# A differential-attention kernel: half of the groups subtracted before the transposes, their magnitudes summed on ScalarE

## The chip, the cores and the metric

The kernel runs on one core of one Trainium2 chip. The metric is the device time of one execution in microseconds. A core has five engines that work through their own queues in order: TensorE (PE in the profile, with its weight loads as PEld), VectorE (DVE), ScalarE (ACT), GpSimd (POOL) and the queue engine SyncE (SP).

## The reference

The input x is 8 sequences of 512 tokens with 128 features. Differential attention with 16 heads of 8 features is followed by a layer norm and a mixture of 8 experts of which each token uses 2. The part that the change touches is the attention:

```
s1 = q @ k1.T * SCALE ; s2 = q @ k2.T * SCALE        # causal, per head
attn = softmax(s1) - sigmoid(lambda) * softmax(s2)
denom = maximum(sum(abs(attn), axis=-1), 1e-6)
out = (attn / denom) @ v
x = layernorm(x + out @ Wo.T)
...
x = layernorm(x + moe(layernorm(x) * gamma + beta))
```

## The kernel before

**Units.** A unit is 32 queries of one sequence `b`; a sequence has 16 units `j`, and unit `j` sees L = 32 (j+1) keys. Four heads make a group, and a group's four heads times 32 queries fill the 128 partitions. So a unit has four groups of [128, L] scores, each twice: set 0 for k1 and set 1 for k2. The tile `et` holds the exponentials of all groups and both sets, as `et[:, g, set, :L]`.

**What happens to a unit.** `scores` puts the scores into PSUM (L342, and a causal mask by L351). `maxima` takes the negated row maximum on VectorE (L364, L372). `exps` takes the exponential on ScalarE and, with it, the row sums (L382). `combine` then does two things for each group: VectorE forms max(e1, c·e2) and sums it along the row into `big` (L408; the elementwise result goes to a tile `junk` that nobody reads), and GpSimd scales e2 by -c in place (L418). Here c is the ratio of the two row sums times sigmoid(lambda), made in `ratios`. The sum of magnitudes needs no subtraction, because |a - b| = 2 max(a, b) - a - b. `transposes` turns both tensors of a group on TensorE into the same place in PSUM, where the second is added to the first (L436), so that the difference comes out of the transposes. `evacuate` copies it to SBUF on ScalarE (L456, L458), and `times_v` multiplies with the values (L468). When four units of a block are done, `reciprocals` forms the denominators from `sums` and `big`.

**Pieces and slots.** A unit with L up to 256 is early: it has two slots (two groups with both sets each) and two pieces, groups (0, 1) and (2, 3). A later unit has four slots (two groups, one set) and four pieces of one group each. A slot is one round of the schedule.

**The order.** The order on each engine is written out by hand, in `round_of`, with manual scheduling: the program issues instructions in exactly this order. A round, for the slot `now` whose scores are there and the slot `ahead` whose scores are next, issues: the product with v of units that are ready; the scores of `ahead`; the evacuation of the transposes of the round before; ScalarE's waiting steps (`on_act`: the tanh of an expert, L815, or the copy of its output, L860, with a store); the maxima of `now`; the transposes of the piece combined the round before; VectorE's waiting steps; the combining of the next piece; the exponentials of `now`; late VectorE steps; then projection, normalisation and routing steps and up to two expert steps (L850, L870), as a pace allows. Score tiles have two buffers in PSUM, the transposes' tile `pt` has one, `et` has three.

**Experts.** They run in chunks of 5 to 7 blocks, some rounds behind the attention; from the third sequence on expert steps stand between the attention's steps.

Of the kernel before, what the change touches and what calls it, by code (L numbers as in the profile page):

```python
# [20 lines left out]
def kernel(  # L21
# [15 lines left out]
    nc = tc.nc  # L37
# [96 lines left out]
    with ExitStack() as actx:  # L134
# [28 lines left out]
        won = aw.tile([P, D], F32, name="won")  # L163
        wo_sb = aw.tile([P, 4, D], F32, name="wo_sb")
        slam = aw.tile([P, NG], F32, name="slam")
        slam1 = aw.tile([P, NG], F32, name="slam1")
        hm = aw.tile([P, 4], F32, name="hm")
        hms = aw.tile([P, 4], F32, name="hms")
# [1 line left out]
        i4 = aw.tile([P, 4, Q], BF16, name="i4")  # L170
        mk = aw.tile([P, Q], BF16, name="mk")
        junk = aw.tile([P, T], F32, name="junk")

        xts = {}

# [47 lines left out]
            )  # L223
        nc.scalar.activation(slam, slam, AF.Sigmoid)
        nc.vector.tensor_scalar(slam1, slam, 1.0, None, ALU.add)
        for h in range(4):
            nc.vector.tensor_scalar_mul(wo_sb[:, h, :], won, hm[:, h : h + 1])

# [86 lines left out]
        class Unit:  # L315


            def __init__(self, b, j, blk):
# [11 lines left out]
                self.et = ep.tile([P, NG, 2, T], F32, tag="et", name=f"et_{b}_{j}")  # L330
                self.aT = self.c2 = None

            def scores(self, slot):
                gp, s = slot
                qb, kT, _ = qkv[self.b]
                L, j = self.L, self.j
                sc = ps_s.tile([P, 2, T], F32, tag="sc", name=f"sc_{self.b}_{j}_{gp}_{s}")
                for si in range(2) if s is None else (s,):
                    lo = 0 if s is not None else si * (T // 2)
                    for gi in range(2):  # L340
                        r = slice(32 * (2 * gp + gi), 32 * (2 * gp + gi) + 32)
                        nc.tensor.matmul(  # L342
                            sc[:, gi, lo : lo + L],
                            lhsT=qb[r, j].rearrange("p h q -> p (h q)"),
                            rhs=kT[r, si, :L],
                            start=True,
                            stop=False,
                        )
                    for gi in range(2):
                        r = slice(32 * (2 * gp + gi), 32 * (2 * gp + gi) + 32)  # L350
                        nc.tensor.matmul(  # L351
                            sc[:, gi, lo + L - Q : lo + L],
                            lhsT=i4[r].rearrange("p h q -> p (h q)"),
                            rhs=mk[r],
                            start=False,
                            stop=True,
                        )
                return sc
# [31 lines left out]
            def ratios(self):  # L390

                sums, jj = self.blk["sums"], self.jj
                c1 = sp.tile([P, NG], F32, tag="c1", name=f"c1_{self.b}_{self.j}")
                nc.vector.tensor_mul(c1, sums[:, 0, jj, :], slam)
                self.c2 = sp.tile([P, NG], F32, tag="c2", name=f"c2_{self.b}_{self.j}")
                r2 = sp.tile([P, NG], F32, tag="r2", name=f"r2_{self.b}_{self.j}")
                nc.vector.reciprocal(r2, sums[:, 1, jj, :])
                nc.vector.tensor_mul(self.c2, c1, r2)

            def combine(self, piece):  # L400

                if self.c2 is None:
                    self.ratios()
                L = self.L
                for g in piece:
                    nc.vector.scalar_tensor_tensor(  # L408
                        junk[:, :L],
                        self.et[:, g, 1, :L],  # L410
                        self.c2[:, g : g + 1],
                        self.et[:, g, 0, :L],
                        ALU.mult,
                        ALU.max,
                        accum_out=self.blk["big"][:, self.jj, g : g + 1],
                    )
                for g in piece:
                    nc.gpsimd.tensor_scalar(  # L418
                        self.et[:, g, 1, :L],
                        self.et[:, g, 1, :L],  # L420
                        self.c2[:, g : g + 1],
                        -1.0,
                        ALU.mult,
                        ALU.mult,
                    )

            def widths(self):
                return [min(P, self.L - P * kb) for kb in range(self.n)]

            def transposes(self, piece):  # L430

                pt = ps_t.tile([P, 4, P], F32, tag="pt", name=f"pt_{self.b}_{self.j}_{piece[0]}")
                for x_, g in enumerate(piece):
                    for kb, kw in enumerate(self.widths()):
                        for k in range(2):
                            nc.tensor.matmul(  # L436
                                pt[:kw, x_ * self.n + kb, :],
                                lhsT=self.et[:, g, k, kb * P : kb * P + kw],
                                rhs=ident,
                                is_transpose=True,  # L440
                                start=(k == 0),
                                stop=(k == 1),
                            )
                return pt

# [30 lines left out]
        def block_tasks(b, i, blk):  # L476
# [7 lines left out]
            def reciprocals():  # L484
                s["oraw"] = op.tile([P, JT, P], F32, tag="oraw", name=f"oraw_{n}")
                nc.scalar.copy(s["oraw"], blk["po"])

                dg = bp.tile([P, JT, NG], F32, tag="dg", name=f"dg_{n}")
                nc.vector.tensor_mul(
                    dg, blk["sums"][:, 0], slam1.unsqueeze(1).to_broadcast([P, JT, NG])  # L490
                )
                nc.vector.scalar_tensor_tensor(dg, blk["big"], 2.0, dg, ALU.mult, ALU.subtract)
                nc.vector.scalar_tensor_tensor(
                    dg, blk["sums"][:, 0], 1e-6, dg, ALU.mult, ALU.max
                )
                rd = bp.tile([P, JT, NG], F32, tag="rd", name=f"rd_{n}")
                nc.vector.reciprocal(rd, dg)
                s["rexp"] = op.tile([P, JT, NG, 32], F32, tag="rexp", name=f"rexp_{n}")
                nc.gpsimd.tensor_copy(s["rexp"], rd.unsqueeze(3).to_broadcast([P, JT, NG, 32]))
# [558 lines left out]
        def round_of(now=None, ahead=None):  # L1058

            nonlocal due, now_at
            for _ in range(len(to_multiply)):
                after_blocks(to_multiply.popleft())
            if ahead:
                ahead["sc"] = ahead["u"].scores(ahead["slot"])
            for _ in range(len(to_evacuate)):
                v, piece, pt = to_evacuate.popleft()
                v.evacuate(piece, pt)
                if piece[-1] == NG - 1:  # L1070
                    to_multiply.append(v)
            run(on_act)
            if now:
                now["u"].maxima(now["slot"], now["sc"])
            for _ in range(len(to_transpose)):
                v, piece = to_transpose.popleft()
                to_evacuate.append((v, piece, v.transposes(piece)))
            run(on_dve)
            left = now["left"] if now else 2
            for _ in range(-(-len(to_combine) // left)):  # L1080
                v, piece = to_combine.popleft()
                v.combine(piece)
                to_transpose.append((v, piece))
            if now:
                now["u"].exps(now["slot"], now["sc"])
                if now["left"] == 1:
                    to_combine.extend((now["u"], piece) for piece in now["u"].pieces)
            run(on_dve_late)
            room = 2
            if misc:  # L1090
                misc.popleft()()
                room -= 1
            if routing:
                step = routing.popleft()
                step()
                room -= step.__name__ == "counts"


            for _ in range(1 if now else 2):
                if moves or gathers:  # L1100
                    (moves or gathers).popleft()()
            if now:
                spent = time_of(2 * now["u"].L * (2 if now["slot"][1] is None else 1))
                now_at += spent
                due += spent * pace
            else:
                due += 2
            while due >= 1 and experts and room:
                experts.popleft()()
                due -= 1  # L1110
                room -= 1
            due = min(due, 4.0)
# [87 lines left out]
```

## Time and profile before

| | |
|---|---|
| median of 3 runs | 1283.44 us (1280.96 to 1287.62) |
| the profiled execution: its own time | 1282.53 us |
| its span in the profile | 1279.5 us |
| TensorE busy | 1169.2 us, 91% |
| VectorE busy | 974.3 us, 76% |
| ScalarE busy | 814.8 us, 64% |
| GpSimd busy | 492.6 us, 38% |
| TensorE's granted clock, mean | 0.937 of full speed |

The profile is one execution, taken by the hardware profiler. A line of its groups names the kernel's line, the engine, the operation, output and inputs with partitions x elements, the count, the busy time in us, the mean duration in ns, and the idle time of the engine just before, with what ended most of it. Tensor names leave out buffer numbers: `sc_None` is the score tile of an early unit's slot, `sc` that of a late one. A wait is put down to the instruction that released it.

### The profile page before, as it was taken

The numbers are of one execution on the slowest core, as the hardware profiler recorded it, in microseconds if no ns is written. First come the engines' busy times: TensorE is split into PE (matmuls) and PEld (weight loads), VectorE is DVE, ScalarE is ACT, GpSimd is POOL, SyncE is SP. The second block draws the span as 40 slices with busy tenths as digits, with TensorE's granted clock in tenths as the row PEclk, the third lists the DMA queues.
The fourth block names the chain that finished last, engine by engine and source line by source line (L and its number), as shares of the span: only waits on it lengthen the run. The fifth ranks groups of instructions, "written<-read, shape, count | busy, mean of one in ns | idle before, by whom it ended". The sixth has DMA issues, their size and how long they took to land.

```text
span 1279.5 us, 31232 instructions
## 1 busy us (share of the span) xinstructions
PE 1169.2 (91%) x10780; PEld 869.9 (68%) x10780; DVE 974.3 (76%) x2981; ACT 814.8 (64%) x2928; POOL 492.6 (38%) x853
## 2 busy tenths in 40 slices
PE   5999998998999899999999989988899899999775
PEld 3666665567767766677767657776667776778665
DVE  3688768587888889968887688869678887787643
ACT  3677766577777677777766656767567655665211
POOL 2243334433322656333336362233444724244300
PEclk8699969799999999999999789999899978999888
DMA  8000000211122121312221122222232323446340
GB/s 241 1 2 2 10 1 22 73 41 52 55 71 63 45 76 42 92 45 72 63 71 43 57 67 88 65 64 69 59 92 77 92 84 100 120 129 174 113 119 24
DMA packets 123996, 88.73 MB, mean 69 GB/s; under 512 B 9920, under 2 KB 108096, under 8 KB 123840
## 3 DMA queue, kind: packets, MB, share of 16 engines
q1 hardware_dynamic: 105856, 72.83, 19.5%
q0 software_dynamic: 3584, 7.35, 2.0%
q10 hardware_dynamic: 14400, 6.57, 1.8%
q8 instruction: 86, 1.41, 0.4%
q14 instruction: 70, 0.57, 0.1%
HBM read 69.02 MB, written 17.69 MB: 68 GB/s over the span
## 4 chain that ended last, share of the span: by engine, by line
PE 65%; DVE 17%; ACT 8%; issue 4%; POOL 3%; DMA 3%; ACTq 0%; SPq 0%; POOLq 0%; DVEq 0%
PE pt L436 20%; PE sc L342 12%; PE sc_None L342 6%; PE po L468 6%; PE pa L850 5%; PE pz L870 5%; ACT et L382 4%; DVE junk L408 3%; DVE nm L372 3%; PE pmo L519 2%; PE py L964 2%; PE pzd L951 2%; DVE nm L364 1%; DMA xs<-xh,row 1%; ACT aT L456 1%
## 5 line engine op out<-in xcount | busy, mean ns | idle before, releaser
L418 POOL TENSOR_SCALAR et<-et,c 128x224 f32<-128x224 f32 (+15 forms) x512 | 266.4, 525 | 495.3 <-DVE junk L408 324.4
L436 PE MATMUL pt<-ident,et 128*128 128x128 f32 (+3 forms) x2560 | 386.4, 291 | 29.5 <-POOL et L418 14.6
L436 PEld LDWEIGHTS pt<-ident,et 128*128 128x128 f32 (+3 forms) x2560 | 274.1, 136 | 148.4 <-issue 45.5
L382 ACT ACTIVATE et<-sc,nm 128x512 f32<-128x512 f32 (+7 forms) x512 | 299.2, 591 | 62.1 <-DVE nm L372 38.9
L372 DVE TENSOR_REDUCE nm<-sc 128x2 f32<-128x576 f32 (+7 forms) x256 | 252.1, 985 | 43.9 <-PE sc L351 43.0
L408 DVE SCALAR_TENSOR_TENSOR junk<-et,c 128x224 f32<-128x224 f32 (+15 forms) x512 | 262.0, 512 | 9.6
L342 PE MATMUL sc<-kT,qb 32*128 32x384 f32 (+7 forms) x1024 | 245.8, 557 | 8.1 <-ACT et L382 6.9
L456 ACT COPY aT<-pt 128x256 f32<-128x256 f32 (+1 forms) x336 | 149.2, 444 | 134.5 <-PE pt L436 131.8
L382 ACT ACTIVATE et<-sc_None,nm 128x256 f32<-128x256 f32 (+7 forms) x512 | 187.1, 378 | 20.1 <-DVE nm L364 9.8
L342 PE MATMUL sc_None<-kT,qb 32*128 32x128 f32 (+7 forms) x1024 | 135.3, 380 | 15.7 <-ACT et L382 15.4
L364 DVE TENSOR_REDUCE nm<-sc_None 128x4 f32<-128x256 f32 (+7 forms) x128 | 96.2, 752 | 40.8 <-PE sc_None L351 40.3
L112 POOL TENSOR_TENSOR l_rs<-l_ve,nhalf 128x1 f32<-128x1 f32 x96 | 60.6, 631 | 167.1 <-DVE l_ve L110 133.2
L342 PEld LDWEIGHTS sc_None<-kT,qb 32*128 32x128 f32 x1024 | 86.5, 210 | 50.2 <-ACT et L382 23.7
L342 PEld LDWEIGHTS sc<-kT,qb 32*128 32x128 f32 x1024 | 78.0, 186 | 57.1 <-ACT et L382 22.5
L468 PE MATMUL po<-aT,vt 128*32 128x128 f32 (+3 forms) x2560 | 107.3, 287 | 0.0
L870 PE MATMUL pz<-xgT,w 128*128 128x128 f32 x728 | 102.7, 287 | 2.6 <-DVE xgT L844 2.1
L382 ACT ACTIVATION_READ_ACCUMULATOR et<-sc_None,nm 128x1 f32 x512 | 104.0, 203 | 0.0
L382 ACT ACTIVATION_READ_ACCUMULATOR et<-sc,nm 128x1 f32 x512 | 102.0, 199 | 0.0
L850 PE MATMUL pa<-w,hT 128*128 128x128 f32 x728 | 99.7, 282 | 0.6 <-ACT ysb L860 0.6
L870 PEld LDWEIGHTS pz<-xgT,w 128*128 128x128 f32 x728 | 93.9, 201 | 6.4 <-DVE xgT L844 3.1
L850 PEld LDWEIGHTS pa<-w,hT 128*128 128x128 f32 x728 | 92.8, 199 | 2.4 <-issue 1.4
L458 ACT COPY aT<-pt 32x128 f32<-32x128 f32 (+5 forms) x288 | 84.6, 294 | 9.8 <-PE pt L436 9.8
(143 smaller groups left out, 1379.1 us busy)
## 6 DMA issues: line engine op xcount, KB each, us to landing
w<-in_w_dram SPq DMA_DIRECT2D x214, 256.0 KB, 3.0
xg<-xs SPq DMA_DIRECT2D x91, 64.0 KB, 3.1
ys<-ysb ACTq DMA_DIRECT2D x91, 64.0 KB, 1.8
xs<-zero SPq DMA_DIRECT2D x2, 1216.0 KB
xt<-in_x_dram SPq DMA_DIRECT2D x8, 256.0 KB, 2.8
out_dram<-ot SPq DMA_DIRECT2D x32, 64.0 KB, 1.6
xs<-zero SPq DMA_DIRECT2D x1, 1344.0 KB, 11.5
xs<-zero SPq DMA_DIRECT2D x1, 1088.0 KB
```

Of the source, the lines that this page charges most:

```text
L342: nc.tensor.matmul(sc[:, gi, lo : lo + L], lhsT=qb[r, j].rearrange("p h q -> p (h q)"), rhs=kT[r, si, :L], start=True, stop=False,)
L364: nc.vector.tensor_reduce(self.nm[:, g, :], sc.rearrange("p g (s l) -> p g s l", s=2)[:, :, :, : self.L], AX.X, ALU.max, negate=True,)
L372: nc.vector.tensor_reduce(self.nm[:, g, s], sc[:, :, : self.L], AX.X, ALU.max, negate=True)
L382: nc.scalar.activation(self.et[:, g, si, : self.L], sc[:, gi, lo : lo + self.L], AF.Exp, bias=self.nm[:, g, si : si + 1], accum_out=self.b ...
L408: nc.vector.scalar_tensor_tensor(junk[:, :L], self.et[:, g, 1, :L], self.c2[:, g : g + 1], self.et[:, g, 0, :L], ALU.mult, ALU.max, accum_ ...
L418: nc.gpsimd.tensor_scalar(self.et[:, g, 1, :L], self.et[:, g, 1, :L], self.c2[:, g : g + 1], -1.0, ALU.mult, ALU.mult,)
L436: nc.tensor.matmul(pt[:kw, x_ * self.n + kb, :], lhsT=self.et[:, g, k, kb * P : kb * P + kw], rhs=ident, is_transpose=True, start=(k == 0) ...
L456: nc.scalar.copy(self.aT[:, g, :full, :], src[:, :, :full, :])
L458: nc.scalar.copy(self.aT[: w[-1], g, full, :], src[: w[-1], :, full, :])
L468: nc.tensor.matmul(self.blk["po"][32 * g : 32 * g + 32, self.jj, :], lhsT=vt[:kw, kb, 32 * g : 32 * g + 32], rhs=self.aT[:kw, g, kb, :], s ...
L850: nc.tensor.matmul(pm[:, 1, :], lhsT=hT[y][:, f, :], rhs=w[y][1][:, f, :], start=(f == 0), stop=(f == NF - 1),)
L870: nc.tensor.matmul(pz[:, f, :], lhsT=w[t][0][:, f * P : (f + 1) * P], rhs=xgT[t], start=True, stop=True,)
```

## The change

For the first two sequences (b = 0 and 1) nothing changes. From the third on, in groups 2 and 3 of every unit:

- VectorE forms the difference itself: its pass now multiplies by a negated ratio (`slams` holds sigmoid(lambda) with the sign turned for groups 2 and 3) and adds, and writes the difference in place over set 0, without a row sum.
- GpSimd's scaling of set 1 is left out.
- TensorE transposes one tensor instead of two.
- ScalarE takes the absolute value of the difference into a scratch tile and sums it into `big`. This stands in `magnitudes`, called in the round directly after the piece's transposes were issued, and so on ScalarE after the evacuations and `on_act` and ahead of the round's exponentials.
- The denominators of these groups take `big` as it is.

```
+        nc.vector.tensor_copy(slams[:, 0:2], slam[:, 0:2])
+        nc.vector.tensor_scalar_mul(slams[:, 2:4], slam[:, 2:4], -1.0)
...
+                self.added = range(NG) if b < 2 else range(2)
...
-                nc.vector.tensor_mul(c1, sums[:, 0, jj, :], slam)
+                nc.vector.tensor_mul(c1, sums[:, 0, jj, :], slam if len(self.added) == NG else slams)
...
                 for g in piece:
+                    added = g in self.added
                     nc.vector.scalar_tensor_tensor(
-                        junk[:, :L],
+                        junk[:, :L] if added else self.et[:, g, 0, :L],
                         self.et[:, g, 1, :L],
                         self.c2[:, g : g + 1],
                         self.et[:, g, 0, :L],
                         ALU.mult,
-                        ALU.max,
-                        accum_out=self.blk["big"][:, self.jj, g : g + 1],
+                        ALU.max if added else ALU.add,
+                        **({"accum_out": self.blk["big"][:, self.jj, g : g + 1]} if added else {}),
                     )
                 for g in piece:
+                    if g not in self.added:
+                        continue
                     nc.gpsimd.tensor_scalar(
...
+            def magnitudes(self, piece):
+                for g in piece:
+                    if g not in self.added:
+                        nc.scalar.activation(
+                            junka[:, : self.L],
+                            self.et[:, g, 0, : self.L],
+                            AF.Abs,
+                            accum_out=self.blk["big"][:, self.jj, g : g + 1],
+                        )
...
-                        for k in range(2):
+                        sets = 2 if g in self.added else 1
+                        for k in range(sets):
...
-                                stop=(k == 1),
+                                stop=(k == sets - 1),
...
+                y = slice(0, NG if b < 2 else 2)
                 nc.vector.tensor_mul(
-                    dg, blk["sums"][:, 0], slam1.unsqueeze(1).to_broadcast([P, JT, NG])
+                    dg[:, :, y],
+                    blk["sums"][:, 0, :, y],
+                    slam1[:, y].unsqueeze(1).to_broadcast([P, JT, y.stop]),
                 )
-                nc.vector.scalar_tensor_tensor(dg, blk["big"], 2.0, dg, ALU.mult, ALU.subtract)
                 nc.vector.scalar_tensor_tensor(
-                    dg, blk["sums"][:, 0], 1e-6, dg, ALU.mult, ALU.max
+                    blk["big"][:, :, y], blk["big"][:, :, y], 2.0, dg[:, :, y], ALU.mult, ALU.subtract
+                )
+                nc.vector.scalar_tensor_tensor(
+                    dg, blk["sums"][:, 0], 1e-6, blk["big"], ALU.mult, ALU.max
                 )
...
                 to_evacuate.append((v, piece, v.transposes(piece)))
+                v.magnitudes(piece)
```

More of the change, by code (lines that the diff above doesn't have):

```diff
@@ L165 @@
         slam = aw.tile([P, NG], F32, name="slam")
+        slams = aw.tile([P, NG], F32, name="slams")
         slam1 = aw.tile([P, NG], F32, name="slam1")
@@ L172 @@
         junk = aw.tile([P, T], F32, name="junk")
+        junka = aw.tile([P, T], F32, name="junka")
         xts = {}
```

## The prediction

> **What bounds the kernel now.** I read the busy shares first, then the stretches of the span, the chain that ended last, the groups of instructions, and at the end the waits. The page's head:
>
> ```profile
> span 1279.5 us, 31232 instructions
> ...
> PE 1169.2 (91%) x10780; PEld 869.9 (68%) x10780; DVE 974.3 (76%) x2981; ACT 814.8 (64%) x2928; POOL 492.6 (38%) x853
> ```
>
> TensorE is busy 91% of the span, which alone proves little. So I cut the span where the changed work lies. The exponentials of the third sequence start at 279 us and those of the last end at 1167 us; the last transposes end at 1182 us. In the busy table by stretches (engine, busy us, instructions; then TensorE's granted clock, DMA share, GB/s):
>
> ```profile
> core 0: us, PE busy (x) PEld busy (x) DVE busy (x) ACT busy (x) POOL busy (x), PEclk, DMA share, GB/s
> 292.00:1181.00 889.00, 838.25 (x8013) 631.20 (x8012) 721.25 (x2203) 605.45 (x2186) 371.56 (x589) 0.97 0.26 76
> ...
> 1181.00:1279.50 98.50, 68.98 (x467) 62.53 (x466) 45.81 (x124) 19.15 (x24) 14.07 (x19) 0.88 0.31 90
> ```
>
> Inside this stretch TensorE is busy 838 of 889 us (94%), VectorE 721 (81%), ScalarE 605 (68%). The last 98 us hold only experts and stores, which the change does not touch. Six sequences in 888 us are 148 us each. The chain that ended last, in the same stretch:
>
> ```profile
> by line: PE pt L436 19.6%; PE sc L342 12.4%; PE pa L850 7.8%; PE pz L870 7.4%; PE po L468 5.9%; PE sc_None L342 5.2%; ACT et L382 4.7%; issue 4.3%; DVE junk L408 3.8%; DVE nm L372 3.1%; PE pmo L519 1.7%; DVE nm L364 1.7%; DMA xs<-xh,row 1.6
> ```
>
> The TensorE lines together hold about two thirds of it; the transposes of L436 alone 19.6%. ScalarE's exponentials hold 4.7%, VectorE's L408 3.8%. The bound is TensorE, with a second, rarer path through ScalarE. One piece of the chain in order of time (start us, duration us, what) shows that second path:
>
> ```profile
> 323.52 0.91 PE pz L870 x8
> ...
> 324.45 0.60 ACT th L815
> 325.05 1.83 ACT et L382 x8
> 326.89 0.04 issue
> 326.93 0.75 PE sc L342 x4
> ```
>
> Here TensorE has finished an expert's matmuls (pz); ScalarE takes its tanh, then eight exponentials (the x8 counts the four and their accumulator reads), and only then is a score buffer free. In this place the change will put ScalarE's new work. The groups that carry the prices (busy us, mean ns of one, idle before):
>
> ```profile
> L418 POOL TENSOR_SCALAR et<-et,c 128x224 f32<-128x224 f32 (+15 forms) x512 | 266.4, 525 | 495.3 <-DVE junk L408 324.4
> L436 PE MATMUL pt<-ident,et 128*128 128x128 f32 (+3 forms) x2560 | 386.4, 291 | 29.5 <-POOL et L418 14.6
> ...
> L382 ACT ACTIVATE et<-sc,nm 128x512 f32<-128x512 f32 (+7 forms) x512 | 299.2, 591 | 62.1 <-DVE nm L372 38.9
> ...
> L408 DVE SCALAR_TENSOR_TENSOR junk<-et,c 128x224 f32<-128x224 f32 (+15 forms) x512 | 262.0, 512 | 9.6
> ...
> L382 ACT ACTIVATE et<-sc_None,nm 128x256 f32<-128x256 f32 (+7 forms) x512 | 187.1, 378 | 20.1 <-DVE nm L364 9.8
> ```
>
> [...] the tanh with constants of 128x512 took 597 ns[...], the exponential of 128x512 with its pointer bias 685 ns[...]. [...] The trace shows only two table loads of 1283 ns, both at the start, and tanh and exp alternate afterwards without one; so I give the new function no load. [...] at 128x256, L408 took 478 ns without and 480 ns with L418 beside it. I count no gain for VectorE from GpSimd's lighter load.
>
> **The change part by part.** It acts in 6 sequences x 16 units x 2 groups = 192 cases; half are in early units (keys 32 to 256, both groups in one round), half in late ones (288 to 512, a group per round).
>
> *TensorE loses 480 transposes.* A sequence has 2560/8 = 320 of L436; two of four groups need one tensor for two, so 80 go, in six sequences 480. The program's order of instructions shows 2080 left. In the timeline a run of eight takes 1.09 us and one takes 0.273, so the spacing is (1.09-0.273)/7 = 0.117 us: 56 us, or 58 at the stretch's clock of 0.97. That is work. On the path, L436 has 19.6% of 889 = 174 us, nearly all in these sequences, and a quarter goes: **-44 us**, the value I take; 58 is the upper end.
>
> *GpSimd loses 192 scalings*, at 525 ns 101 us. It is 38% busy, so the work is free; what counts is who waited:
>
> ```profile
> ACT aT L456 <- PE pt L436: 131.8, 166, 2.9
> ...
> PEld pt L436 <- POOL et L418: 18.9, 22, 2.5
> ...
> PE pt L436 <- POOL et L418: 14.6, 18, 2.3
> ```
>
> TensorE's matmul and weight-load queues stood 18.9+14.6 = 33.5 us for L418; of that 2/4 x 6/8 = 12.6 us at most goes. The chain's pieces name L418 for 8.5 us; half of it is **-4 us**. The transposes then wait for VectorE, which comes before GpSimd anyway.
>
> *VectorE keeps its 192 passes*, adding in place, without the accumulator read. From start to start two passes with reads were 0.50 us for 0.45 of work, so 0.05 x 192 = 10 us of VectorE's time; of the 34 us that L408 has on the chain a twentieth: **-2 us**. The two set-up instructions and the changed operands of the block's denominator are within a microsecond and lie beside TensorE's work.
>
> *ScalarE gains 192 activations with an accumulator read.* The nearest row, the exponentials: 96 x 378 + 96 x 591 ns = 93 us. [...] The reads (about 200 ns) overlap the next activation (exponentials of 0.44 us start every 0.43), so 0 to 0.1 us more each, up to 19 us. I take 93, or 15.5 us per sequence. ScalarE's work with its DMA issues was 106 of 148 us per sequence, so 42 were idle, mostly waiting for TensorE (the aT line above alone 131.8 us in the whole run). The work fits in sum. Its own new wait, for VectorE's addition, should end early: that pass stands in VectorE's queue ahead of the maxima for which the exponentials behind it wait anyway. No DMA issue moves. What costs is where it stands: behind the tanh or the expert's copy, ahead of the exponentials; queued behind it are the exponentials, and behind those the next scores and VectorE's combining. From the timeline I took, for 285 rounds of these sequences, the time from the end of a round's exponentials to the start of the scores that reuse its buffer: median 1.14 us, under 0.3 us in 59 rounds (ScalarE decides there), 0.3 to 0.65 in 23. Half of the rounds get new work, on average (8 x 2 x 0.378 + 16 x 0.591)/24 = 0.65 us. So 30 x 0.65 = 19 us; by the chain, which goes 33 times through exponentials, 16 x 0.65 = 11. I take **+15**, and for the second class 12 x 0.3 = **+4**.
>
> *Sum:* -44-4-2+15+4 = -31 us. The profiled execution had a span of 1279.5 and its own time was 1282.53, 3.0 more: 1248.5+3.0 = 1251.5. The median of the runs, 1283.44, is 0.9 above that execution, so 1252.4, rounded **1252 us**. Each 0.08 us of ScalarE exposed per activation moves this by 15 us.
>
> **The rivals.** Within 0.5% (1277 to 1290) is about what a measurement of this kernel cannot tell from no change.
>
> *All relief comes through (0.22).* The activations fit into ScalarE's waits for pt wholly: 58 us off, up to 6 more from GpSimd and VectorE: 1220 to 1238. For it: the median slack of 1.14 us exceeds 0.65. Against: expert rounds, where ScalarE cannot use its idle time, because the new work stands behind the tanh that it is waiting for.
>
> *The relief is eaten by the next limit (0.18).* With 138 us of TensorE, 120 of VectorE and 122 of ScalarE per sequence, rounds alternate between bounds, the short ones no longer fill, or TensorE is granted less clock: 0.97 to 0.93 would cost 838 x 0.04 = 34 us, as much as the gain. 1266 to 1290. For it: VectorE was already the busiest engine in 45 of 287 rounds. Against: TensorE was it in 221.
>
> *ScalarE becomes the bound, slower (0.10).* Place: between expert copy and exponentials. Price: if all 93 us are exposed while the path gets back 44 to 58 us, 1283+35 to 1283+49, about 1325; it decides from 0.30 us exposed per activation (58/192), half of its price. For it: a quarter of the rounds has no slack. Against: the other three quarters.
>
> That it doesn't do what it says is excluded by the instruction order, which has the 480 transposes fewer and 192 activations more.
>
> **How the numbers follow.** The forecast has 0.50, with 1238 to 1266 of its own (path gain 44 to 58, ScalarE's cost 11 to 35). Faster by over 0.5%: 0.50+0.22+half of the third, 0.09 = 0.81; same 0.09; slower 0.10. The range 1226 to 1280 leaves out the slower case (0.10), a part of the full relief (0.06) and the end of the third (0.04).
>
> **What would show it.** Right: 2080 transposes on L436's successor, its share of the chain at about 15% of the stretch; ScalarE 605+93 = some 700 us in it; the new activation at 0.38 and 0.59 us; more waits of score weight loads for exponentials, against 23.7+22.5 = 46 us of them now. Wrong: activations with longer spacing than 0.7 us, a table load inside the loop, TensorE's clock below 0.95 in the stretch, or VectorE's lines taking over the chain from TensorE.

## The result

The changed kernel is slower: 1329.37 us median of four runs (1323.16 to 1339.36) against 1282.20 of the kernel before, a ratio of 1.039 with a 95% interval of 1.029 to 1.049. The prediction of 1252 us, range 1226 to 1280, was wrong, in sign too. Executions of one kernel differ by some 3%, so a ratio with its interval compares only the fast runs of each kernel, those within 1.5% of its fastest, while medians are over all its runs. The profiled execution took 1323.16 us, the lowest of the four. Its page begins:

```profile
span 1321.4 us, 30229 instructions
...
PE 1173.5 (89%) x10300; PEld 858.9 (65%) x10300; DVE 960.9 (73%) x2791; ACT 884.7 (67%) x3312; POOL 392.6 (30%) x661
```

TensorE issued 480 matmuls fewer (10300 for 10780), and yet it was busy 1173.5 us for 1169.2 before. Fewer instructions with about the same busy time means that they took longer on average. The busy table of the stretch with the attention of the last six sequences (engine, busy us, instructions; TensorE's granted clock, DMA share, GB/s):

```profile
core 0: us, PE busy (x) PEld busy (x) DVE busy (x) ACT busy (x) POOL busy (x), PEclk, DMA share, GB/s
292.00:1225.00 933.00, 843.71 (x7596) 622.71 (x7596) 709.37 (x2020) 677.98 (x2577) 272.33 (x399) 0.90 0.25 73
```

The stretch is 933 us where it was 889, and the column to read is the granted clock: 0.90 where it was 0.97. The chain in the same stretch:

```profile
by line: PE pt L458 15.1%; PE sc L348 10.6%; ACT et L388 10.6%; PE pa L877 6.5%; PE pz L897 6.3%; PE po L490 5.6%; issue 5.3%; PE sc_None L348 4.7%; ACT junka L441 3.8%; PE pmo L546 2.2%; DVE junk L416 2.1%; ACT aT L478 1.8%; DVE nm L378 1.
```

The transposes' share fell from 19.6% to 15.1%, as forecast, but ScalarE's exponentials rose from 4.7 to 10.6%, and the new activation (junka) holds 3.8%. The groups of the page give the same picture, and so do the waits below them (us in total, times, longest us):

```profile
L458 PE MATMUL pt<-ident,et 128*128 128x128 f32 (+3 forms) x2080 | 349.2, 306 | 29.2 <-ACT aT L478 12.1
...
L388 ACT ACTIVATE et<-sc,nm 128x512 f32<-128x512 f32 (+7 forms) x512 | 298.0, 589 | 45.4 <-DVE nm L378 29.2
...
L441 ACT ACTIVATE junka<-et 128x32 f32<-128x32 f32 (+7 forms) x192 | 82.7, 430 | 16.6 <-ACT ysb L887 9.3
```

Before, the score weights (the weight loads of the score matmuls) had these waits for exponentials:

```profile
PEld sc_None L342 <- ACT et L382: 23.7, 35, 1.5
...
PEld sc L342 <- ACT et L382: 22.5, 48, 1.5
```

In the changed kernel:

```profile
PEld sc L348 <- ACT et L388: 46.0, 74, 1.5
PEld sc_None L348 <- ACT et L388: 45.2, 49, 2.2
```

The 192 activations took 430 ns on average, 82.7 us, below the price that I took. The transposes' mean rose from 291 to 306 ns, though their work is the same. The score weights waited 46.0+45.2 = 91.2 us for exponentials, twice the 46.2 of before.

Where the clock went can be read from the 40 slices of the page, in tenths of full speed. The kernel before, then the changed one:

```profile
PEclk8699969799999999999999789999899978999888
```

```profile
PEclk8599969797999888999998687987799989899888
```

In steps of 0.5 us the clock of these two executions is 1.00 or 0.50, but for the steps in which it changes; the tenths are mixtures. Time at half clock in the attention of the last six sequences (from the first exponential of the third sequence to the last one's end): 61 us of 888 in 8 episodes before, 181 us of 929 in 29 episodes after. The rest of the two executions is alike: 279 and 281 us ahead of that stretch, 112 us behind it in both.

How an episode begins is seen where one unit's keys fall from 512 to 32, in the changed kernel. First busy times in stretches of 3.4 us, then a few lines of the timeline (start, duration; in brackets the idle time before, and who ended it):

```profile
424.80:428.20 3.40, 2.99 (x40) 2.71 (x37) 3.04 (x16) 3.00 (x11) 0.00 (x0) 1.00 0.67 176
428.20:431.60 3.40, 1.89 (x27) 1.50 (x22) 3.33 (x9) 3.19 (x21) 2.25 (x2) 1.00 0.07 19
431.60:435.00 3.40, 2.80 (x28) 2.41 (x32) 3.06 (x15) 1.34 (x3) 0.00 (x0) 0.52 0.00 0
```

```profile
427.94 0.60 ACT L441 ACTIVATE junka<-et 128x480 f32<-128x480 f32 x1 [0.40 <-ACT ysb L887]
...
428.55 0.27 ACT L388 ACTIVATE et<-sc_None,nm 128x32 f32<-128x32 f32 x1
...
429.33 0.29 ACT L388 ACTIVATE et<-sc_None,nm 128x32 f32<-128x32 f32 x1
...
429.76 0.44 PE L348 MATMUL sc_None<-kT,qb 32*128 32x64 f32 x4 [1.43 <-ACT et L388]
...
430.43 1.09 PE L458 MATMUL pt<-ident,et 128*128 128x128 f32 x8
...
432.20 1.97 PE L458 MATMUL pt<-ident,et 128*128 128x128 f32 x8 [0.68 <-ACT aT L478]
```

An activation of 0.60 us with the keys of an earlier, long unit stands ahead of short exponentials; TensorE waits 1.43 us for the last of them. The activation is part of this gap and not all of it: VectorE, too, is busy 3.33 of the 3.4 us. In the stretch from 428.2 to 431.6 TensorE is busy 1.89 of 3.4 us. Then the clock is 0.52, and eight transposes that took 1.09 us take 1.97.

### The profile page after: what moved, and what is told of

It is laid out like the page before. It is cut to its first block, busy times and chain, and to the rows that moved or that the text cites. A ratio compares the mean times of both kernels' runs of the same rounds, so it can differ in the third digit from the quotient of the medians.

```text
span 1321.4 us, 30229 instructions
## 1 busy us (share of the span) xinstructions
PE 1173.5 (89%) x10300; PEld 858.9 (65%) x10300; DVE 960.9 (73%) x2791; ACT 884.7 (67%) x3312; POOL 392.6 (30%) x661
## 4 chain that ended last, share of the span: by engine, by line
PE 59%; ACT 16%; DVE 14%; issue 5%; POOL 2%; DMA 2%; ACTq 1%; SPq 0%; POOLq 0%; DVEq 0%
PE pt L458 17%; PE sc L348 11%; ACT et L388 8%; PE sc_None L348 6%; PE po L490 6%; PE pa L877 5%; PE pz L897 5%; ACT junka L441 3%; PE pmo L546 2%; PE py L991 2%; PE pzd L978 2%; DVE junk L416 2%; DVE nm L378 2%; ACT aT L478 2%; DVE nm L370 1%
## 5 line engine op out<-in xcount | busy, mean ns | idle before, releaser
L458 PE MATMUL pt<-ident,et 128*128 128x128 f32 (+3 forms) x2080 | 349.2, 306 | 29.2 <-ACT aT L478 12.1
L458 PEld LDWEIGHTS pt<-ident,et 128*128 128x128 f32 (+3 forms) x2080 | 232.9, 142 | 151.6 <-issue 49.7
L428 POOL TENSOR_SCALAR et<-et,c 128x32 f32<-128x32 f32 (+15 forms) x320 | 168.6, 532 | 482.3 <-DVE junk L416 360.2
L348 PE MATMUL sc<-kT,qb 32*128 32x384 f32 (+7 forms) x1024 | 250.2, 566 | 28.2 <-ACT et L388 25.6
L348 PE MATMUL sc_None<-kT,qb 32*128 32x128 f32 (+7 forms) x1024 | 142.4, 394 | 34.4 <-ACT et L388 33.5
L416 DVE SCALAR_TENSOR_TENSOR junk<-et,c 128x32 f32<-128x32 f32 (+15 forms) x320 | 163.4, 511 | 7.8
L348 PEld LDWEIGHTS sc_None<-kT,qb 32*128 32x128 f32 x1024 | 90.0, 218 | 71.8 <-ACT et L388 45.2
L490 PE MATMUL po<-aT,vt 128*32 128x128 f32 (+3 forms) x2560 | 114.4, 302 | 0.0
L877 PE MATMUL pa<-w,hT 128*128 128x128 f32 x728 | 107.4, 296 | 0.8 <-ACT ysb L887 0.8
L877 PEld LDWEIGHTS pa<-w,hT 128*128 128x128 f32 x728 | 100.9, 214 | 2.7 <-issue 1.4
L441 ACT ACTIVATE junka<-et 128x32 f32<-128x32 f32 (+7 forms) x192 | 82.7, 430 | 16.6 <-ACT ysb L887 9.3
```

Source lines behind the costliest of these rows:

```text
L348: nc.tensor.matmul(sc[:, gi, lo : lo + L], lhsT=qb[r, j].rearrange("p h q -> p (h q)"), rhs=kT[r, si, :L], start=True, stop=False,)
L416: nc.vector.scalar_tensor_tensor(junk[:, :L] if added else self.et[:, g, 0, :L], self.et[:, g, 1, :L], self.c2[:, g : g + 1], self.et[:, g ...
L428: nc.gpsimd.tensor_scalar(self.et[:, g, 1, :L], self.et[:, g, 1, :L], self.c2[:, g : g + 1], -1.0, ALU.mult, ALU.mult,)
L441: nc.scalar.activation(junka[:, : self.L], self.et[:, g, 0, : self.L], AF.Abs, accum_out=self.blk["big"][:, self.jj, g : g + 1],)
L458: nc.tensor.matmul(pt[:kw, x_ * self.n + kb, :], lhsT=self.et[:, g, k, kb * P : kb * P + kw], rhs=ident, is_transpose=True, start=(k == 0) ...
L490: nc.tensor.matmul(self.blk["po"][32 * g : 32 * g + 32, self.jj, :], lhsT=vt[:kw, kb, 32 * g : 32 * g + 32], rhs=self.aT[:kw, g, kb, :], s ...
```

## The experiments

Each was compared with the kernel before on the same chip. The table gives medians and ratio with interval, and from one profiled execution of each, for the attention of the last six sequences: its length, the time at half clock, and the length less half of that time. The last column is an estimate of the length without clock losses; it takes all halved time as TensorE-bound and so removes rather too much. The runs give a measured price. Every run has its span and mean clock on record, and so its time at half clock in the whole execution; over 104 runs of the kernel before (1261 to 1299 us), the span grew by 0.42 us for each us at half clock (95% interval 0.40 to 0.44). "At the measured price" below means 0.42 us for each us at half clock, applied to the means over all runs of a kernel; these are estimates.

| kernel | median us | ratio [95%] | length | at half clock | length less half of it |
|---|---|---|---|---|---|
| before | 1282 | | 888 | 61 | 858 |
| changed | 1329 | 1.039 [1.029, 1.049] | 929 | 181 | 839 |
| transposes twice | 1304.5 | 1.023 [1.014, 1.031] | 902 | 51 | 877 |
| no magnitudes | 1276.5 | 1.000 [0.997, 1.003] | 879 | 116 | 821 |
| magnitudes alone | 1301.9 | 1.022 [1.010, 1.033] | 909 | 51 | 884 |
| magnitudes late | 1305.8 | 1.023 [1.014, 1.031] | 915 | 191 | 820 |
| fillers | 1300.4 | 1.013 [0.996, 1.030] | 910 | 113 | 853 |
| GpSimd adds | 1335.0 | 1.039 [1.024, 1.055] | 941 | 215 | 833 |
| GpSimd adds, fillers | 1311.6 | 1.027 [1.014, 1.040] | 919 | 133 | 852 |
| one group | 1286.6 | 1.005 [1.002, 1.009] | 883 | 75 | 845 |
| late, transposes twice | 1286.1 | 1.004 [1.001, 1.007] | 894 | 65 | 862 |
| late, fillers | 1284.4 | see text | 897 | 116 | 839 |
| late, own filler | 1282.8 | 1.000 [0.997, 1.004] | 893 | 82 | 852 |
| late, one group | 1260.5 | 0.984 [0.978, 0.989] | 869 | 61 | 838 |

**Theories.** A: ScalarE's new work delays the exponentials, TensorE stands, and its clock is halved because it stands; fewer transposes are a relief. B: the transposes that are gone leave TensorE so idle that its clock is halved, and that eats the relief; ScalarE's work is secondary.

### Four kernels that separate the two

*Transposes twice.* The changed kernel, with each transpose of a changed group issued twice.

```
-                        for k in range(sets):
+                        for k in range(2):
...
+                                lhsT=self.et[:, g, k if g in self.added else 0, kb * P : kb * P + kw],
...
+                                start=(k == 0 or g not in self.added),
...
```

> As the changed kernel, but in the changed groups TensorE turns the difference twice into the same place, so TensorE has its old number of transposes back; everything else stays. Theory A (ScalarE's new work delays the exponentials, TensorE stands, and its clock is halved because it stands; fewer transposes are a relief): slower than the changed kernel, 1340 to 1385 us. Theory B (the missing transposes themselves leave TensorE too idle, so the clock is halved; ScalarE's work is secondary): faster than the changed kernel, 1280 to 1310, half-clock time in the attention of the last six sequences back from 181 to under 100 us.

Measured 1304.5 us: every one of its six runs (up to 1309.3) was below every run of the changed kernel (from 1323.2), with 480 transposes of useless work more. The busy table of its attention stretch (columns as above):

```profile
281.00:1183.00 902.00, 832.86 (x8056) 626.24 (x8056) 706.77 (x2020) 678.56 (x2588) 273.60 (x402) 0.97 0.25 73
```

The clock is 0.97 again and half-clock time 51 us. A would have it slower; B's forecast came.

*No magnitudes.* The changed kernel without ScalarE's new work; VectorE's addition writes a plain row sum instead, so this kernel does not compute the reference's denominators.

```
-                        **({"accum_out": self.blk["big"][:, self.jj, g : g + 1]} if added else {}),
+                        accum_out=self.blk["big"][:, self.jj, g : g + 1],
...
-                v.magnitudes(piece)
```

> As the changed kernel, but ScalarE's magnitudes are left out; VectorE's addition writes its plain row sum into the same place instead, so that the denominators of these groups are not those of the reference. TensorE and GpSimd keep their relief. Theory A: the whole relief shows, 1225 to 1250 us, half-clock time near the 61 us of the kernel before. Theory B: no better than before, 1270 to 1300, half-clock time over 120 us.

Measured 1276.5 us over 20 runs, ratio 1.000 with an interval of 0.997 to 1.003. The relief of TensorE alone brings nothing that can be measured:

```profile
281.00:1160.00 879.00, 813.46 (x7595) 598.27 (x7594) 706.01 (x2209) 603.52 (x2214) 274.65 (x402) 0.93 0.26 75
```

The clock is 0.93 and the half-clock time 116 us, nearly twice that of before, though just short of the 120 that B had named. Without it the stretch would be 821 for 858 us: a relief of 37 us is there. At the measured price it is 36 us over all runs, and the clock takes nearly all of it.

*Magnitudes alone.* The kernel before with 192 activations more. They read an exponential and so, other than in the change, do not wait for VectorE.

```
+                    if self.b >= 2 and g >= 2:
+                        nc.scalar.activation(
+                            junka[:, : self.L], self.et[:, g, 0, : self.L], AF.Abs,
+                            accum_out=self.blk["extra"][:, self.jj, g : g + 1],
+                        )
...
```

> The kernel before, with 192 extra activations (absolute value with a row sum, into tiles that nobody reads) in the same places and groups as in the change; nothing is taken from TensorE or GpSimd. Theory A: ScalarE's delay comes in full, 1330 to 1390 us, with the clock halved for 120 us or more of the attention of the last six sequences. Theory B: the clock stays as before because TensorE keeps its work, 1285 to 1315.

Measured 1301.9 us, 20 more than the median of before (28 by the ratio, 1.022), clock 0.97, half-clock time 51 us: as B had it.

```profile
281.00:1189.00 908.00, 835.04 (x8050) 627.08 (x8048) 718.61 (x2207) 678.86 (x2583) 373.36 (x592) 0.97 0.25 73
```

So neither part alone makes the loss. By the ratios ScalarE's work alone costs 2.2%, the relief alone nothing, and both together 3.9%; the 1.7% between is uncertain by about 1.5%. The time at half clock in the whole execution, as the mean of all runs, is clearer: 159 us before, 166 with magnitudes alone, 234 without magnitudes, 306 in the change, with 95% intervals of 7 to 27 us. The two parts add 82 us when apart and 147 us together: the rest came only with both parts in the kernel.

*Magnitudes late.* The same work, queued behind the round's exponentials.

```
-                v.magnitudes(piece)
+                to_measure.append((v, piece))
...
                 now["u"].exps(now["slot"], now["sc"])
...
+            while to_measure:
+                v, piece = to_measure.popleft()
+                v.magnitudes(piece)
```

> As the changed kernel, but the magnitudes stand behind the round's exponentials in ScalarE's queue instead of ahead of them. Theory A: most of the loss goes, 1270 to 1310 us, since the exponentials start earlier in their own round, though what stands in the next round comes later. Theory B: no difference to the changed kernel beyond 10 us, 1318 to 1340.

Measured 1305.8 us, 24 less than the changed kernel: here A's number came, and B, which had forecast at most 10, missed. But the clock did not recover (0.90, 191 us at half):

```profile
281.00:1194.00 913.00, 843.52 (x7566) 617.96 (x7566) 702.68 (x2013) 673.30 (x2577) 273.29 (x401) 0.90 0.25 72
```

Less half of that time the stretch is 820 us, what it is without magnitudes (821). So place decides what ScalarE costs in delay: behind the exponentials about nothing by this estimate, and 7 us at the measured price. Yet the half-clock time is 191 us where it is 116 without magnitudes, so even from there ScalarE's work reaches the clock. One trace of this is that the transposes' weight loads waited 39.4 us for ScalarE's copies at L480, and 21.5 us without magnitudes; whether that wait makes the difference was not tried.

### Cheap work for the clock, other places, other doses

*Fillers.* The changed kernel with one bf16 matmul ahead of each transpose that the transpose overwrites.

```
+                        if g not in self.added:
+                            nc.tensor.matmul(
+                                pt[:, x_ * self.n + kb, :], lhsT=identb, rhs=identb, start=True, stop=True
+                            )
```

> The changed kernel, and ahead of each transpose of a changed group one bf16 matmul of 128x128 by the identity into the same place, which the transpose then overwrites: 480 fillers that compute nothing. Theory B (fewer transposes leave TensorE too idle, so its clock is halved): any cheap work will do; half-clock time in the attention of the last six sequences falls from 181 us to 60 to 120, and the time from 1329 to 1295 to 1315 us although work was added. Theory A (ScalarE's work alone): 480 more instructions can only cost, 1329 to 1345. If only transposes keep the clock, the time stays near 1329 with 181 us at half clock.

Measured 1300.4 us, between 1292.7 and 1318.2, below every run of the changed kernel; clock 0.94, half-clock time 113 us for 181. So bf16 matmuls, too, brought back a part of the clock; it did not take transposes.

```profile
281.00:1188.00 907.00, 831.12 (x8034) 617.19 (x8033) 705.14 (x2013) 674.84 (x2580) 271.89 (x401) 0.94 0.26 73
```

*GpSimd adds.* VectorE and the denominators as before; GpSimd scales and then adds.

```
+                    if g not in self.added:
+                        nc.gpsimd.tensor_tensor(
+                            self.et[:, g, 0, :L], self.et[:, g, 0, :L], self.et[:, g, 1, :L], ALU.add
+                        )
```

> The kernel before, with one addition more on GpSimd in the changed groups: GpSimd scales set 1 and then adds it to set 0 in place, TensorE turns one tensor, VectorE sums the maxima as before, and ScalarE gets nothing. Theory B: the relief of TensorE is taken back by its clock as without the magnitudes, 1270 to 1295 us with over 100 us of half clock. Without a clock effect: 1240 to 1260. If GpSimd's second pass comes too late for the transposes: 1300 or more.

Measured 1335.0 us, the third case: GpSimd's additions took 763 ns each, and the transposes waited for them. The wait of the weight loads and the stretch:

```profile
PEld pt L459 <- POOL et L434: 54.7, 67, 2.6
```

```profile
281.00:1222.00 941.00, 855.79 (x7594) 627.41 (x7592) 753.04 (x2209) 605.92 (x2213) 517.77 (x780) 0.89 0.25 70
```

A wait for an addition is new (before, these weight loads waited 18.9 us for GpSimd's scaling), and with it come 215 us at half clock. At the measured price the clock takes 62 us; without that the kernel would be 13 us faster than the one before, and the kernel without magnitudes 36, so some 23 us go to the late additions.

*GpSimd adds, with fillers.*

> The kernel with GpSimd's addition, and ahead of each transpose of a changed group one bf16 filler matmul that the transpose overwrites. Theory B: under 90 us at half clock and 10 to 25 us less than without the fillers, 1250 to 1275 us, perhaps below the kernel before. Otherwise equal or slower than without them.

Measured 1311.6 us with 133 us at half clock: 23 us less than without fillers, as B said, but over its 90 us at half clock and not in the expected range of times, which had been set before the late additions were known.

*One group.* `range(3)` for `range(2)` in `added`, and the slices to match.

> The changed kernel with the change in one group of four instead of two (240 transposes fewer, 96 activations more). Half the load of both kinds. If losses simply add up: half of the change's 47 us, 1300 to 1310. If ScalarE's delays and TensorE's gaps bring one another over the limit at which the clock is halved: less than half, 1285 to 1298, with half-clock time under 100 us.

Measured 1286.6 us with 75 us at half clock: 5 us lost where half of the change's loss would be 24. The loss is not proportional: the half-clock time of the stretch rose by 14 us (75 for 61), where the whole change brought 120. That a limit is behind it was my assumption; the runs do not show one.

*Late, and transposes twice.*

> Magnitudes behind the exponentials, as in the late kernel (1306 us, 191 us at half clock in the attention of the last six sequences), and every transpose of a changed group done twice, as in the kernel with doubled transposes. If position and clock are two separate causes: half-clock time back to 50 to 80 us and 1270 to 1290 us. If doubled transposes only helped because they delay TensorE behind ScalarE: no gain on the late kernel, 1300 to 1320.

Measured 1286.1 us, 65 us at half clock. Each remedy alone took back about 24 us; both together take back 43 of 47. They add up, so the delay by place and the loss by missing transposes are two causes and not one.

*Late, with fillers.*

> Magnitudes behind the exponentials, and one bf16 filler matmul ahead of each transpose of a changed group that the transpose overwrites. If position and clock are separate: half-clock time 90 to 130 us, 1270 to 1290 us, perhaps just below the kernel before. If the fillers only add work: 1306 to 1325.

Measured 1284.4 us median of 20 runs, which spread from 1252.8 to 1298.4. One run far below the others makes the ratio useless here (0.990, resting on two runs), so I take no difference from it. The median and the 116 us at half clock lie within what was expected of separate causes; the profiled execution took 1291.3 us.

*Late, own filler.* One filler of 128x512 at the end of a round, into a PSUM tile of its own.

```
+            if now and now["u"].b >= 2 and any(p[-1] >= 2 for _, p in to_transpose):
+                fill = ps_m.tile([P, 512], F32, tag="pm", name=...)
+                nc.tensor.matmul(fill, lhsT=identb, rhs=wide, start=True, stop=True)
```

> Magnitudes behind the exponentials, and at the end of each round after which a changed group is turned one bf16 filler matmul of 128x512 into a PSUM tile of its own that nobody reads (144 of them[...]): it stands just ahead of the scores, where TensorE waits for ScalarE. If the filler runs in idle time and keeps the clock: 1265 to 1285 us with under 130 us of half clock. If the place doesn't matter and it takes the expert steps' PSUM tiles: 1290 to 1320.

Measured 1282.8 us, ratio 1.000 [0.997, 1.004], 82 us at half clock. In the trace a filler took 0.38 us. With these 144 instructions the half-clock time is nearly as low as with 480 doubled transposes (65 us), but with two groups no filler brought a clear gain on the kernel before.

*Late, one group.*

> The change in one group of four instead of two, and its magnitudes behind the round's exponentials: the two remedies that each took back most of the loss, together. If position and clock are separate causes, half of the relief (some 18 us) stays against half of ScalarE's delay behind the exponentials (a few us) and about 10 us from 75 to 90 us at half clock: 1265 to 1278 us, below both kernels. If one group already costs the clock as much as it gives: 1278 to 1290.

Measured 1260.5 us, ratio 0.984 [0.978, 0.989]: below both kernels, below the expected range too, and with no filler.

```profile
281.00:1148.00 867.00, 810.49 (x7805) 603.30 (x7804) 705.66 (x2108) 635.76 (x2389) 325.23 (x497) 0.96 0.26 76
```

The clock is 0.96 and the half-clock time 61 us, as before; the expectation had allowed for more. The stretch is 869 us for 888: 19 us stay, about half of the 37 us that the whole relief was worth at full clock.

## Why the prediction was wrong

**What held.** 480 transposes went and 192 activations came, at 430 ns, without a table load of their own: the trace has two, of 1283 ns each, in the first 23 us, as before. The relief at full clock was forecast as -44-4-2 = -50 us and is about -37 (no magnitudes, 821 for 858). ScalarE's exposure was forecast as +15+4 = 19 us; the estimate at full clock gives 839-821 = 18 inside the change and 884-858 = 26 on the kernel before. Scores that started within 0.3 us of the exponentials that free their buffer rose from 59 of 285 rounds to about 110. Together: 839-858 = -19 us for -31 forecast. Over all runs, at the measured price, it is -36 for the relief and +22 for the activations, -14 us together.

**The step that failed** is the one that is not in the sum: the transposes removed were priced in time at the clock of before. 119 us more at half clock, worth up to 60 us, turn -19 into the +41 by which the stretch grew (929-888). The mean of all runs rose by 48 us; with 147 us more at half clock, the measured price divides this into 62 us for the clock and the -14 above. The rival in which the next limit eats the relief had named "TensorE is granted less clock", from 0.97 to 0.93 for 34 us, as a thing beside the forecast. It was a consequence of it: taking work from TensorE brought 116 us at half clock for 61, and delaying what it waits for, on top of that, 181; alone, the delay brought none (51). By the same view the clock was 0.90, below the 0.95 that the text had named as a sign of error. I had read "TensorE 94% busy" as a reserve to be relieved; it was also what held the clock (0.90 in the change, 0.97 with its transposes doubled).

**The slower rival** had the right number, about 1325, for the wrong reason. It put all the loss on activations ahead of exponentials. That mechanism alone costs 20 to 28 us (magnitudes alone), less than its price of 93.

**A smaller reading.** That GpSimd does not slow VectorE was read at 128x256 alone. Of the 512 passes of L408 in the kernel before, 24 took over 60 ns more than is usual for their shape, 23 of these beside a pass of GpSimd over `et`, `qb` or `rexp`. They cost 7 us of VectorE's time in the whole execution, so the account does not change.

**TensorE's clock** is what the prediction treated as given. In the changed kernel it fell after stretches in which TensorE was busy for half to four fifths of the time, not idle (0.48 to 0.79, last section).

What stays open: how the halving follows from TensorE's gaps, and by which wait the late magnitudes still reach the clock.

## What to carry to other kernels

When TensorE is the bound and its clock follows its activity, as here (0.97 before, 0.90 changed, 0.97 with the transposes doubled), price a relief of TensorE twice: the time saved, and the time at half clock that comes with it (116 us without magnitudes, 61 before). New work on another engine belongs behind whatever TensorE waits for next (24 us less here), even if that engine has idle time in sum. And a dose matters: in the better place half of the change gained 1.6%, where the whole lost 2.2% there and 3.9% in its own place.

## What the runs showed of the hardware

In the profiled execution of the changed kernel the clock fell to half 29 times in the attention of the last six sequences. In the 3.4 us ahead of each fall TensorE was busy for 0.48 to 0.79 of the time, where over the whole stretch of 933 us it was busy for 0.90 (843.71 us). In the kernel before it fell 8 times, after 3.4 us with shares of 0.06 to 0.86, where over 889 us TensorE was busy for 0.94.

So in these two executions the clock was lost after gaps in TensorE's work, and 35 of the 37 times TensorE had still been busy for more than half of those 3.4 us. The ends of matmuls are modelled by the profile, so the shares are rough. The share at which the clock is lost or comes back is not shown by them.

Bf16 matmuls of the identity held the clock too, though not as fully as the doubled transposes: 113 us at half clock with them and 51 with the transposes, for 181 in the change.
